# Background work between the score passes, and four kinds of small memory-layer operations on ScalarE

## Chip, cores and metric

The kernel runs on one core of a Trainium2 chip. The metric is device time in microseconds (us) for one execution, lower is better; for one core it is the time of that core. Engines are called as the profile calls them: PE is TensorE (PEld its weight loads), DVE is VectorE, ACT is ScalarE, POOL is GpSimd, SP is SyncE, whose queue issues nearly all transfers here.

## What is computed

Four transformer-like layers follow each other on one sequence of 2048 tokens of width 128, all in float32. Each half layer is `x = x + f(layernorm(x))`:

- L0: 16 heads of width 8 over the whole sequence, then a GELU network of 512.
- L1: 16 heads of width 64 over the whole sequence, then a gated network of 384. This attention is the longest stage.
- L2: attention of every token over itself and its two neighbours, then one of eight experts per token.
- L3: a memory layer and a mixture of experts. The memory layer cuts the sequence into 32 chunks of 64 tokens. In every chunk the gradient of a small two-layer network is taken at the state that the chunk before left, and three first-order recurrences along the tokens (with the gates `alpha`, `eta`, `theta`) make of it the state of the next chunk. So the 32 chunks are one serial chain:

```python
for c0 in range(0, S, CHUNK):
    g = _grad_fn(W_state, k[:, sl], v[:, sl]) * GRAD_SCALE
    ...
    (S_state, W_state), Wtraj = jax.lax.scan(step, (S_state, W_state), xs)
    ...
    outs.append(jnp.einsum('bto,btpo->btp', h, W2t))
```

The neighbours in L2 wrap round at the sequence's ends, so a block of tokens needs an edge token of the next block; those edge tokens are computed by themselves ahead of their blocks (the "late edge tokens", lines 1318 to 1374, which the change leaves as they are).

## The kernel before

**Stages.** L0 runs first, up to about 908 us. Then `l1_attn` (line 1066) runs the L1 attention as 40 units: five blocks of queries (512, 384 + 4 edge tokens, 512, 384 and 256 tokens) times eight pairs of heads. A unit has 16 steps, one for each 128 keys. In a step PE makes the scores of two heads, in four passes that add up in PSUM (query high part with key high part, query low part with key high part, query high part with key low part, and a row that subtracts the maximum); ACT takes the exponential into a `P` tile (line 1171); POOL adds the `P` tiles up into `acg`, or DVE into `acd` for four of the 16 steps (`do_sum`, line 1099); and two steps at a time PE multiplies `P` with the values (`do_pv`, line 1082). The maxima come one to two units early: extra products (`mi<-km,qh`) that DVE reduces into `mx` (`max_upto`, line 493).

**Background.** As soon as a block of queries is through all eight pairs of heads, its tokens can go on through the L1 network, L2 and L3. That is done by Python generators, called parts: `stage_a` to `stage_b2` for L1's network and L2, `stage_c` (line 1501) for what a block of 128 tokens needs ahead of the chunk chain, `chunk` (line 1630) for the chain, `stage_d` for its output, `stage_g`, `stage_e0`, `s_lane` and `stage_e1` for the experts. Each part is cut at every `yield` into pieces. What it yields tells the planner what comes next: a number is how many PSUM banks the next piece takes, "same" that it goes on on the same engine, "T" that it holds a product that needs no new bank, a fraction (only `T["late"]` = 0.3) how long to wait.

**What sets the order.** The program is scheduled by hand: each engine does its instructions strictly in the order in which the Python code emits them. A planner keeps a modelled clock for every engine (`note`, line 96) and `fill` (line 246) emits pieces whose inputs are ready by it. `Part.may` (line 202) is the gate; it also refuses a piece when ACT's or DVE's clock is too far ahead of PE's, and, during the attention, a piece that takes a bank unless five more banks stay free. `fill(lim, "t")` emits only pieces without a bank and without a product, and stops after `lim` us of PE's clock:

```python
if only and (self.banks or self.pe):
    return False
...
if len(free) < k + (0 if tail else leave[0]) or free[k - 1] > clk["T"] + T["slack"]:
```

All eight PSUM banks are one pool during the attention (`ps=dict(mx=8)`). In the loop over steps (lines 1136 to 1186) every second step, "last", calls a full `fill()` after its exponentials and another after its products with the values; each other step calls `fill(T["lim"], "t")` after its exponentials (line 1178). So the background comes in at three places in two steps. After the last unit `drain` (line 262) emits what is left; the stretch from there to the end is called the tail below.

**The lines that the prediction's steps touch.** In `stage_c`: the copies between `cb` (tile `sA`) and `hist` (lines 1526 and 1531), the copies of one column from `et` (tile `sB`) into `de` (tile `dE`) and from `om` (tile `sA`) into `do` (tile `dO`), each ahead of a memset of the column copied (lines 1600 to 1603), and the two products into `g1` (tile `gq`, lines 1619 to 1622). `stage_e0` (line 1876) takes a PSUM bank for a block's expert sum, which is given back only when all 13 weight tiles of the block have been through the lanes. Because a helper records every operation, the profile puts all of them on line 147, and they are told apart by their tiles.

Of the kernel before, what the change touches and what calls it, by code (L numbers as in the profile page):

```python
# [14 lines left out]
ALU = mybir.AluOpType  # L15
# [13 lines left out]
CH = 64  # L29
NCH = S // CH  # L30
ATANH = (1.0000000039388743, 0.3333315796754013, 0.20012426861749952, 0.13980709417165652, 0.14087328632693624)
T = dict(lead0=22, more0=4, mgap=0.4, pvq=2, lim0=0.5, fq=(3,), pl=-0.5, pr=1.0, tlow=2, tback=3, late=0.3, pvp="mx", mxp="mx", ex=(1280, 1792, 2047), low=1, lows='ge', keep=1, leave=5, pvn=2, sp=0, rdy=40., eu=2, qg=(22, 16, 10), em=2, el=6, sem=0.2, same=1.2, tsame=3.0, order="hdmBbAaEcCeg", ps=dict(mx=8), dma=2.3, slack=0.1, lim=0.6, backlog=2.5, lead=(10, 8, 6), pp=9, dve=(6, 7, 14, 15), qp=(1, 1), lanes=2, xl=5,
         QB=[(0, 512, 512), (512, 384, 388), (896, 512, 512), (1408, 384, 384), (1792, 256, 256)])


# [35 lines left out]
def body(ctx: ExitStack, tc: tile.TileContext, x, pa, pb, pc, pi, pd, pr, pr0, pe, pw, out):  # L71
# [16 lines left out]
    leave = [0]  # L88
# [92 lines left out]
    mxp = ["mx"]  # L181
# [12 lines left out]
    class Part:  # L194
# [24 lines left out]
        def step(self):  # L219
            piece[0] = clk["T"]  # L220
            r = next(self.gen, "end")
            self.same = r == "same"
            self.ready = 0.0 if self.same else piece[0] + (r if type(r) is float else 0.0)
            self.pe = r == "T"
            self.banks = r if type(r) is int else 0
            self.seen = len(emitted) if r is False else -1
            if r == "end":
                emitted.add(self.key)
            return r != "end"
# [16 lines left out]
    def fill(lim=None, only=""):  # L246

        t0 = clk["T"]
        while clk["T"] - t0 < (lim or T["lim"]):
            kept[0] = 0  # L250
            h = next((h for h in helpers if h.may(only)), None)
            if h:
                if not h.step():
                    helpers.remove(h)
                continue
            st = next((s for s in parts if s.may(only)), None)
            if st is None:
                return
            if not st.step():
                parts.remove(st)  # L260
# [20 lines left out]
    def mm(o, lhsT, rhs, start=True, stop=True, **kw):  # L281
        return te.matmul(o, lhsT, rhs, start=start, stop=stop, **kw)
# [740 lines left out]
    def stage_wo(qb, part):  # L1023

        t0, tn, n = QB[qb]
        yield 1
        ps = mi()
        for p in range(2 * part, 2 * part + 2):
            mm(ps[:, :n], C("wo", p * 128, 128), O.pop(p)[:, :n], start=(p % 2 == 0), stop=(p % 2 == 1))
            yield  # L1030
        if part == 0:
            w = l1w.tile([128, 512], F32, name="wac", tag="wac", bufs=1)
            se.activation(w[:, :n], ps[:, :n], AF.Identity, bias=bo1)
            rel(ps)
            wacc[qb] = w
            return
        w = wacc[qb]
        ve.tensor_tensor(w[:, :n], w[:, :n], ps[:, :n], ALU.add)
        rel(ps)
        if part < NP1 // 2 - 1:  # L1040
            return
        del wacc[qb]
        yield 1
        c0, nt = t0 // 128, tn // 128
        t = mi()
        for i in range(nt):
            te.transpose(tok(t, i), tok(w, i), ident)
        yield
        ve.tensor_tensor(xs[:, c0:c0 + nt, :], xs[:, c0:c0 + nt, :],
                         t[:, :tn].rearrange("p (c d) -> p c d", d=128), ALU.add)  # L1050
        rel(t)
        emitted.add(("x", qb))
        if n != tn:
            ne = len(EXTRA)
            xm = edge_x[0] = sm.tile([ne, 128], F32, name="xm", tag="xm", bufs=1)
            for i, t in enumerate(EXTRA):
                sy.dma_start(xm[i:i + 1, :], xs[t % 128:t % 128 + 1, t // 128, :])
            yield 1
            t = mi()
            te.transpose(t[:ne, :128], w[:, tn:tn + ne], ident)  # L1060
            yield
            ve.tensor_tensor(xm, xm, t[:ne, :128], ALU.add)
            rel(t)
            emitted.add("xm")

    def l1_attn():
# [15 lines left out]
        def do_pv(g, pts, v):  # L1082
            u, k = divmod(g, 16)
            n = QB[units[u][0]][2]
            if k == 0:
                pv[u] = take([T["pvp"]])
            for e in range(2):
                mm(pv[u][64 * e:64 * e + 64, :n], v[:, k % SPC, 64 * e:64 * e + 64], pts[e][:, :n],
                   start=(k == 0), stop=(k == 15), par=(e == 1))
            if k == 15:  # L1090
                accs = acc.pop(u)
                if u:
                    need(("o", u - 1))
                o = opool.tile([128, 512], F32, name="o", tag="o")
                se.copy(o[:, :n], pv[u][:, :n])
                rel(pv.pop(u))
                ends.append((u, o, accs))
# [38 lines left out]
        for g in range(16 * U):  # L1136
            u, k = divmod(g, 16)
            qb, p = units[u]
            n = QB[qb][2]
            if k == 0:  # L1140
                need(("m", u))
                need(("ql", u))
            if u + 2 < U:
                if k == 1 and units[u + 2][1] == 0:
                    need(("q", u + 1))
                    u_loadx(units[u + 2][0])
                if k == T["qp"][n <= 256] and u + 2 >= EU:
                    helper(("q", u + 2), u_qprep(u + 2))
            if k == 2 and 1 < u + 1 < U:
                need(("q", u + 1))  # L1150
                helper(("ql", u + 1), u_qlow(u + 1))
            if k % SPC == 0:
                ka, v = nxt.pop(0)
                g2 = g + 2 * SPC
                if g2 < 16 * U:
                    nxt.append(u_loadk(g2 // 16, (g2 % 16) // SPC))
            last = len(prev) == T["pvn"] or g == 0
            if not last:

                max_upto(max_at(g + 16 + LEAD[n] + 1))  # L1160
            pts = []
            ks = slice((k % SPC) * 128, (k % SPC) * 128 + 128)
            pss = [take(["mx"]) for _ in range(2)]
            ops = ((ka[:, 0, ks], qhh[u]), (ka[:, 0, ks], qlt[u % 2]), (ka[:, 1, ks], qhh[u]), (onr, mbt[u % 2]))
            for i, (a, b) in enumerate(ops):
                for e in range(2):
                    rows = slice(64 * e, 64 * e + 64)
                    mm(pss[e][:, :n], a[rows], b[rows, :n], start=(i == 0), stop=(i == 3), par=e and 0.02)
            for e in range(2):
                pt = pp.tile([128, 512], F32, name="P", tag="P")  # L1170
                se.activation(pt[:, :n], pss[e][:, :n], AF.Exp)
                rel(pss[e])
                pts.append(pt)
            if last:
                max_upto(max_at(g + 16 + LEAD[n] + 1))
                fill()
            else:
                fill(T["lim"], "t")
            if prev:
                do_sum(*prev[-1])  # L1180
            if len(prev) == T["pvn"]:
                while prev:
                    do_pv(*prev.pop(0))
                fill()
            do_merge()
            prev.append((g, pts, v))
        do_sum(*prev[-1])
# [313 lines left out]
    def stage_c(b):  # L1501
# [6 lines left out]
        ps = mi()  # L1508
# [14 lines left out]
            se.activation(th[:, k, :], pa_[:, 32 * k:32 * k + 32], AF.Tanh, scale=0.5, accum_out=s3[:, k:k + 1])  # L1523
        rel(ps)
        yield from wait(("hist", b - 1))
        ve.tensor_copy(cb[:, 0:3], hist)
        yield
        y = lt([128, BN3], "sB" + v)
        tap = lambda j, lo=0, hi=128: C("ctap", j, 1)[lo:hi]
        ve.tensor_scalar(y, cb[:, 0:BN3], tap(0), C("cb"), ALU.mult, ALU.add)  # L1530
        ve.tensor_copy(hist, cb[:, BN3:BN3 + 3])
        emitted.add(("hist", b))
        yield "same"
        for j in (1, 2):
# [62 lines left out]
                                ident[0:64, 0:64].unsqueeze(1).to_broadcast([64, BC3, CH]), ALU.mult, ALU.mult)  # L1597
        yield "same"
        ve.tensor_scalar(fl(om), ps[0:64, :BN3], -0.05 / 32, 0.95, ALU.mult, ALU.add)
        ve.tensor_copy(de[32:64, :, 0:1], et[32:64, :, 0:1])  # L1600
        ve.memset(et[:, :, 0:1], 0.0)
        ve.tensor_copy(do[0:32, :, 0:1], om[0:32, :, 0:1])
        ve.memset(om[:, :, 0:1], 0.0)
        yield "same"
        ve.tensor_tensor_scan(fl(h_), fl(et), fl(imp), 0.0, ALU.mult, ALU.add)
# [11 lines left out]
        yield "same"  # L1617
        ve.tensor_tensor_scan(ab, fl(om), fl(do), 0.0, ALU.mult, ALU.add)
        for r, t, k in ((slice(0, 64), ch(ab), 0), (slice(32, 64), do, 32)):
            ve.tensor_tensor(g1[r, :, k:k + 32], i1[r].unsqueeze(1).to_broadcast([r.stop - r.start, BC3, 32]),  # L1620
                             last(t)[r].to_broadcast([r.stop - r.start, BC3, 32]), ALU.mult)
        yield "same"
        qab = d["qab"] = lt([64, BN3], "qab", 3)
        ge.tensor_tensor(qab, qd_, ab, ALU.mult)
        kcs = d["kcs"] = lt([64, BC3, 2, 32], "kcs", 2)
# [4 lines left out]
    def chunk(b, c):  # L1630
# [46 lines left out]
        ve.tensor_tensor(ef, pf, v2f, ALU.subtract)  # L1677
        ve.tensor_tensor(e2, pt, kvt[:, c, 1, :], ALU.subtract)
        ve.scalar_tensor_tensor(u, tht, 2.0, u, ALU.mult, ALU.add)
        yield  # L1680
        mm(da, ef, w2)
        se.activation(j1, e2, AF.Square, accum_out=rr[:, 1:2])
        acs = lt([64, 2, 32], "acs", 1, l3c)
# [437 lines left out]
```

## Time and profile before

Three runs took 2908.26, 2917.2 and 2914.99 us; the median is 2914.99 us.

| | before |
|---|---|
| profiled execution, its own time | 2916.98 us |
| span in the profile | 2915.2 us |
| mean granted PE clock | 0.946 |
| busy: PE, DVE, ACT, POOL | 2681.3, 2247.1, 1552.2, 1365.5 us |
| attention steps of L1: first and last `mi<-mbt,onr` product | 907.9 and 2533.3 us |
| tail, from there to the end of the span | 382 us |
| share of PE and of DVE in the chain that ended last | 61% and 24% |

A unit issues 32 products `mi<-mbt,onr`, so counting them in the trace gives the start of each unit: unit 17 begins at 1551 us, unit 26 at 1976 us. The background is thin up to unit 16 and thick from there on.

A profile is of one execution. "PEclk" in it is the clock that PE was granted, 1.00 being full speed. A busy PE that runs at half speed shows as busy.

### The profile page before, as it was taken

The page shows a single profiled execution, that of the slowest core. Times are in us where ns is not written, and L with a number is a line of the kernel's source. Part 1 is how long each engine was busy: PE and PEld are TensorE (multiplying, and loading weights), DVE is VectorE, ACT ScalarE, POOL GpSimd, SP SyncE. Part 2 cuts the span into 40 slices and gives each one's busy share as a digit, 9 for nine tenths or more (in the row PEclk, how much of TensorE's full clock was granted, in tenths as well). Part 3 has the DMA queues.
Part 4 walks back from the last instruction along what each step waited for, and adds up shares of the span by engine and source line. Part 5 has one row for each costly group of instructions (what it writes and reads, how often), then busy time and mean ns, then how long its engine had stood idle before and what let it go on. Part 6 is the DMA issues. An engine that isn't in the chain of part 4 may idle for free.

```text
span 2915.2 us, 50126 instructions
## 1 busy us (share of the span) xinstructions
PE 2681.3 (92%) x16719; PEld 1361.4 (47%) x16719; DVE 2247.1 (77%) x4860; ACT 1552.2 (53%) x3932; POOL 1365.5 (47%) x1601
## 2 busy tenths in 40 slices
PE   7999999999988899999999999899889998879898
PEld 1222232222234444455554444455545565556676
DVE  7899888998643767777777778787788888787765
ACT  1788887887964454544444444344344344333444
POOL 3400110201114777766765766466556556433454
PEclk9999999999988999999999999999999999777879
DMA  6311231230225333344443333233233444222344
GB/s 146 74 28 17 52 109 18 73 91 16 79 83 179 100 112 114 120 120 122 139 133 95 97 97 96 81 106 105 92 96 114 122 121 116 79 57 75 80 112 117
DMA packets 247751, 275.82 MB, mean 95 GB/s; under 512 B 95747, under 2 KB 183330, under 8 KB 247366
## 3 DMA queue, kind: packets, MB, share of 16 engines
q1 hardware_dynamic: 246630, 272.43, 33.9%
q8 instruction: 133, 2.18, 0.3%
q14 instruction: 124, 1.02, 0.1%
q10 hardware_dynamic: 864, 0.20, 0.0%
HBM read 229.97 MB, written 42.28 MB: 93 GB/s over the span
## 4 chain that ended last, share of the span: by engine, by line
PE 61%; DVE 24%; ACT 6%; issue 4%; DMA 3%; POOL 1%; SPq 0%; ACTq 0%; POOLq 0%; DVEq 0%
PE mi L147 61%; DVE mx L147 8%; DVE acd L147 3%; ACT P L147 3%; DVE xn L147 1%; DVE xs L147 1%; DVE sB L147 1%; DMA rcd<-rc 1%; DVE gt L147 1%; DMA rb<-rcd 1%; ACT kf L147 1%; DVE hb L147 1%; ACT kh L147 1%; DVE bst L147 1%; DVE sG L147 1%
## 5 line engine op out<-in xcount | busy, mean ns | idle before, releaser
L147 DVE TENSOR_REDUCE mx<-mi 128x1 f32<-128x512 f32 (+1 forms) x2080 | 1318.8, 682 | 458.9 <-PE mi L147 447.5
L147 ACT ACTIVATE P<-mi 128x512 f32<-128x512 f32 (+3 forms) x2304 | 1118.3, 554 | 916.9 <-PE mi L147 891.9
L147 POOL TENSOR_TENSOR acg<-acg,P 128x512 f32<-128x512 f32 (+3 forms) x800 | 858.0, 1100 | 278.3 <-ACT P L147 277.9
L147 PE MATMUL mi<-P,ka 128*64 128x512 f32 (+3 forms) x2560 | 531.2, 537 | 1.9 <-ACT P L147 1.9
L147 PE MATMUL mi<-qh,ka 64*128 64x512 f32 (+3 forms) x2560 | 480.8, 363 | 25.1 <-DVE mx L147 13.7
L147 PE MATMUL mi<-kop,qop 48*128 48x512 bf16 x1024 | 347.5, 404 | 24.6 <-DVE mx L147 12.3
L147 PE MATMUL mi<-qop,kop 50*128 50x512 bf16 x1024 | 316.6, 389 | 27.1 <-ACT P L147 24.7
L147 PE MATMUL mi<-P,vop 128*32 128x512 f32 x2048 | 303.3, 618 | 13.9 <-ACT P L147 13.9
L147 PEld LDWEIGHTS mi<-qh,ka 64*128 64x128 f32 x2560 | 265.0, 189 | 94.4 <-issue 29.5
L147 PE MATMUL mi<-km,qh 64*128 64x512 f32 x1024 | 270.7, 459 | 36.3 <-DVE mx L147 28.8
L147 PEld LDWEIGHTS mi<-P,ka 128*64 128x64 f32 x2560 | 160.1, 140 | 244.2 <-issue 209.1
L147 PE MATMUL mi<-ql,ka 64*128 64x512 f32 (+3 forms) x1280 | 241.7, 354 | 0.0
L147 PE MATMUL mi<-mbt,onr 64*128 64x512 f32 (+3 forms) x1280 | 238.1, 351 | 0.4 <-DMA mbt<-mb 0.4
L147 POOL TENSOR_SCALAR vep<-mv 128x2 f32<-128x2 f32 (+1 forms) x24 | 5.5, 229 | 494.1 <-DVE mv L147 494.1
L147 PEld LDWEIGHTS mi<-km,qh 64*128 64x128 f32 x1024 | 118.6, 188 | 188.4 <-DVE mx L147 84.7
L147 PEld LDWEIGHTS <-kop 50*128 50x128 bf16 x1024 | 63.5, 95 | 303.6 <-issue 280.1
L147 POOL TENSOR_TENSOR acg<-P 128x512 f32<-128x512 f32 (+3 forms) x80 | 88.0, 1120 | 230.9 <-ACT P L147 135.0
L147 PEld LDWEIGHTS mi<-mbt,onr 64*128 64x128 f32 x1280 | 133.7, 189 | 11.2 <-DMA mbt<-mb 1.0
L147 PEld LDWEIGHTS mi<-ql,ka 64*128 64x128 f32 x1280 | 130.4, 189 | 13.5
L147 PEld LDWEIGHTS <-qop 48*128 48x128 bf16 x1024 | 73.0, 95 | 97.2 <-issue 82.8
L147 PEld LDWEIGHTS mi<-P,vop 128*32 128x32 f32 x2048 | 55.4, 109 | 119.4 <-issue 90.6
L147 POOL TENSOR_TENSOR kl<-kf,kh 128x512 f32<-128x512 f32 x32 | 40.9, 1277 | 111.5 <-ACT kh L147 83.0
(510 smaller groups left out, 3516.6 us busy)
## 6 DMA issues: line engine op xcount, KB each, us to landing
ka<-kvd SPq DMA_DIRECT2D x320, 384.0 KB
km<-khd SPq DMA_DIRECT2D x159, 256.0 KB
khd<-kh SPq DMA_DIRECT2D x32, 256.0 KB
kvd<-kh SPq DMA_DIRECT2D x32, 256.0 KB
kvd<-kl SPq DMA_DIRECT2D x32, 256.0 KB
kvd<-vt SPq DMA_DIRECT2D x16, 512.0 KB
w3s<-in_pw_dram SPq DMA_DIRECT2D x38, 192.0 KB
ka<-in_pw_dram SPq DMA_DIRECT2D x35, 192.0 KB
```

Of the source, the lines that this page charges most:

```text
L147: r = f(*a, **k)
```

## The change

Four things are changed, and nothing that is computed:

1. In the attention loop the parts' pieces without products may be emitted at many more places: after the first three of the four score passes, after the exponentials, after each step's product with the values, and after the full fill. Each such call has a limit of 9 us of PE's clock in place of 0.6. The full fills stay. The old call on the steps between is gone (its branch never runs).
2. Three kinds of piece that begin with a product are now marked so that these calls leave them out: the second product of `stage_wo`, the product `da` in `chunk`, and any piece after a fractional wait (the last products of a lane).
3. In `stage_c`, four copies and the products into `g1` go from DVE to ACT. [...]
4. After them the part yields plainly in place of "same".

```diff
-            self.pe = r == "T"
+            self.pe = r == "T" or type(r) is float
...
-            yield
+            yield "T" if p % 2 == 0 else 0
...
                     mm(pss[e][:, :n], a[rows], b[rows, :n], start=(i == 0), stop=(i == 3), par=e and 0.02)
+                if T["tf"] and i in T["ti"]:
+                    fill(9.0, "t")
...
-            else:
-                fill(T["lim"], "t")
+            elif 0:
+                fill()
+            if T["tf"]:
+                fill(9.0, "t")
             if prev:
                 do_sum(*prev[-1])
             if len(prev) == T["pvn"]:
                 while prev:
                     do_pv(*prev.pop(0))
+                    if T["tf"]:
+                        fill(9.0, "t")
                 fill()
+                if T["tf"]:
+                    fill(9.0, "t")
...
-        ve.tensor_copy(cb[:, 0:3], hist)
+        se.copy(cb[:, 0:3], hist)
...
-        ve.tensor_copy(hist, cb[:, BN3:BN3 + 3])
+        se.copy(hist, cb[:, BN3:BN3 + 3])
...
-        ve.tensor_copy(de[32:64, :, 0:1], et[32:64, :, 0:1])
+        se.copy(de[32:64, :, 0:1], et[32:64, :, 0:1])
         ve.memset(et[:, :, 0:1], 0.0)
-        ve.tensor_copy(do[0:32, :, 0:1], om[0:32, :, 0:1])
+        se.copy(do[0:32, :, 0:1], om[0:32, :, 0:1])
         ve.memset(om[:, :, 0:1], 0.0)
...
-            ve.tensor_tensor(g1[r, :, k:k + 32], i1[r].unsqueeze(1).to_broadcast([r.stop - r.start, BC3, 32]),
-                             last(t)[r].to_broadcast([r.stop - r.start, BC3, 32]), ALU.mult)
-        yield "same"
+            for c in range(BC3):
+                se.mul(g1[r, c, k:k + 32], i1[r], last(t)[r, c])
+        yield
...
         ve.scalar_tensor_tensor(u, tht, 2.0, u, ALU.mult, ALU.add)
-        yield
+        yield "T"
         mm(da, ef, w2)
```

The values added to the table of constants are `ti=(0, 1, 2)` and `tf=1`.

More of the change, by code (lines that the diff above doesn't have):

```diff
@@ L31 @@
 ATANH = (1.0000000039388743, 0.3333315796754013, 0.20012426861749952, 0.13980709417165652, 0.14087328632693624)
-T = dict(lead0=22, more0=4, mgap=0.4, pvq=2, lim0=0.5, fq=(3,), pl=-0.5, pr=1.0, tlow=2, tback=3, late=0.3, pvp="mx", mxp="mx", ex=(1280, 1792, 2047), low=1, lows='ge', keep=1, leave=5, pvn=2, sp=0, rdy=40., eu=2, qg=(22, 16, 10), em=2, el=6, sem=0.2, same=1.2, tsame=3.0, order="hdmBbAaEcCeg", ps=dict(mx=8), dma=2.3, slack=0.1, lim=0.6, backlog=2.5, lead=(10, 8, 6), pp=9, dve=(6, 7, 14, 15), qp=(1, 1), lanes=2, xl=5,
+T = dict(ti=(0, 1, 2), tf=1, lead0=22, more0=4, mgap=0.4, pvq=2, lim0=0.5, fq=(3,), pl=-0.5, pr=1.0, tlow=2, tback=3, late=0.3, pvp="mx", mxp="mx", ex=(1280, 1792, 2047), low=1, lows='ge', keep=1, leave=5, pvn=2, sp=0, rdy=40., eu=2, qg=(22, 16, 10), em=2, el=6, sem=0.2, same=1.2, tsame=3.0, order="hdmBbAaEcCeg", ps=dict(mx=8), dma=2.3, slack=0.1, lim=0.6, backlog=2.5, lead=(10, 8, 6), pp=9, dve=(6, 7, 14, 15), qp=(1, 1), lanes=2, xl=5,
          QB=[(0, 512, 512), (512, 384, 388), (896, 512, 512), (1408, 384, 384), (1792, 256, 256)])
```

## The prediction

> **What bounds the kernel now.** I read the totals first: PE is busy 92% of the span, so PE is the bound in name. Then the busy time by stretch: units 17 to 25, units 26 to 39, and the tail. Columns: start and end, length, then busy time of PE, PEld, DVE, ACT and POOL, the granted clock, the DMA share, GB/s.
>
> ```profile
> 1551.00:1976.00 425.00, 398.72 (x2353) 208.75 (x2349) 342.99 (x651) 184.44 (x459) 269.53 (x249) 0.98 0.32 96
> 1976.00:2533.00 557.00, 512.63 (x3788) 316.21 (x3787) 448.15 (x1109) 229.75 (x810) 329.75 (x455) 0.94 0.37 107
> 2533.00:2915.00 382.00, 328.30 (x1687) 247.06 (x1687) 277.41 (x1043) 156.90 (x641) 164.65 (x272) 0.80 0.36 87
> ```
>
> PE stands idle 425.0 - 398.7 = 26 us, 44 us and 54 us in the three, and loses by its clock 425 x 0.02 = 8 us, 557 x 0.06 = 33 us and 382 x 0.20 = 76 us. So 26 + 44 + 8 + 33 = 111 us of the attention with background, and 130 us of the tail, are not PE at its speed. The two losses belong together, as one stall shows. The timeline has DVE at three small operations that took 3.59 us (a `sB` operation of this form has a mean of 0.354 us), then PE that waits for `sA`, their successor:
>
> ```profile
> 1845.76 3.59 DVE L147 SCALAR_TENSOR_TENSOR sB<-sB,sA 128x32 f32<-128x32 f32 x3
> ...
> 1849.87 0.53 PE L147 MATMUL mi<-ident,s 128*64 128x128 f32 x2 [3.02 <-DVE sA L147]
> ```
>
> The granted clock of the next two 10 us was 0.83 and 0.86, after 1.00: a stall of 3 us was paid once as a stall and again, some 20 x 0.155 = 3 us, as clock.
>
> What PE waits for in the attention with background: the waits of PE alone in units 26 to 39 begin with
>
> ```profile
> PE mi L147 <- DVE mx L147: 15.6, 15, 3.0
> ```
>
> and for units 17 to 25 the same row has 17.9 us. Those 33.5 us of the 70 are waits for a PSUM bank that DVE has yet to reduce; the other 37 us are mostly waits for background results, nearly all from DVE. So DVE's lateness, through PE, is what a change can win here.
>
> Last, the rows of the operations that the change moves (ns minimum, median, maximum):
>
> ```profile
> L147 DVE COPY dE<-sB x16: 158/158/2592, 1857.4 to 2798.3; 32x2 f32<-32x2 f32 x16
> ...
> L147 DVE TENSOR_TENSOR gq<-i,ab x16: 216/217/754, 1861.6 to 2800.9; 64x64 f32<-64x64 f32 x16
> L147 DVE TENSOR_TENSOR gq<-i,dO x16: 215/530/3132, 1861.8 to 2801.1; 32x64 f32<-32x64 f32 x16
> ```
>
> The reader is to see that an operation of 0.2 us sometimes takes 2 to 3 us. It works no longer; it is held up while POOL is busy (the second product stands just behind POOL's `qab`, which reads the same tile).
>
> **Part 1: DVE to ACT.** Summed over the 16 calls of `stage_c`, the six removed DVE operations take 3.6 and 5.2 us (`hist`), 6.8 (`dE`), 3.9 (`dO`), 4.7 and 17.4 (`gq`): 41.6 us, of which 26.0 before 2533 us (nine calls) and 15.6 in the tail (seven). At their minima they would take 16 x (0.15 + 0.15 + 0.16 + 0.16 + 0.22 + 0.22) = 17 us; the other 25 us are hold-ups.
> In the attention the gain is between 0 (DVE was idle anyway: it waits 130 us for `mi` between 1551 and 2533) and all 26. I take half, **-13**, since DVE is busy 81% there and PE's waits are for DVE.
> ACT gets four copies and four products a call. Nearest rows: ACT's `ce` copies at 0.18 to 0.19 us, its products by a scale 0.20 (`ce`) to 0.32 us (`en`); so 4 x 0.19 + 4 x 0.26 = 1.8 us, 16 us in nine calls. ACT is busy 414 of 982 us there and waits 463 us for PE's scores, so its time costs nothing by itself; without that cover it would cost the 16.
> The new wait is DVE's: the memsets of `et` and `om` may not run until ACT has copied the column, and behind them on DVE stand the scans and the `mx` reductions that free PE's banks. It is no less than a copy and its hand-over, 0.3 us; with a pair of exponentials (2 x 0.55 us) ahead of it on ACT, 1.5 us. I take 0.5 a call, nearer the first, since the new places put the copy ahead of a step's exponentials: 9 x 0.5, **+4** (ends 3 and 14). `hist` needs no hand-over: ACT writes and reads it, and SP and POOL are not passed by any of these.
> In the tail the removed operations stand on the chain itself: 2.6 us of `dE` at 2531 and 0.4, 0.4, 1.7, 2.4 and 0.2 us of `gq`, together 7.7: **-7**. New waits there 7 x 0.5, **+3**.
>
> [...]
>
> **Part 2: the new places.** In the order of the two programs nothing differs in L0 and little in the first units; the background matmuls, counted by unit, are 157 in both up to unit 16; then 207 before and 293 after in units 17 to 25, 488 and 396 in units 26 to 39, 882 and 888 in the tail. DVE's background operations go from 308, 756 and 992 to 424, 570 and 958. So the background starts earlier and ends no earlier: work is moved from units 26 to 39 into units 17 to 25, and what is left for the tail is the same. Six matmuls of about 0.3 us less in the attention are **-2**, back in the tail as +2.
> What can be won is stalls. A DVE or ACT piece goes in as soon as it is ready, while a product still waits for a full fill; so between the piece and its product more foreground stands. No row shows this. At best the 37 us of waits for background results and half of the 41 us of lost clock vanish (-57); at worst ACT pieces ahead of exponentials delay `P`, for which PE waits 1.1 us now, and DVE pieces ahead of `mx` double the 33.5 us of bank waits (+34). I take a fifth of the first end, **-12**, since the waits to be shortened are the larger half.
>
> **Part 3: what the early start brings with it.** Since the first blocks reach `stage_g` early, `stage_e0` of block 0 is emitted in unit 26 in the changed order (before: in the tail), and it holds one of eight PSUM banks to the tail. Counted at the start of each step, 2.6 banks are held in units 26 to 29 against 2.2, and 2.5 against 1.8 in units 34 to 39. PE's bank waits after unit 26 are 15.6 us: from 0 (banks suffice) to double, with half of the 33 us of lost clock added (+32). I take **+6**.
> The chain of chunks enters the tail later: `stage_c` of block 7 was done in unit 39 and is now done after the last unit, and the tail has one `stage_c` and 0.8 `chunk` more (448 against 380 and 576 against 550 operations), two `stage_g` less. A chunk in the tail took (2847.6 - 2540.8) / 17 = 18 us by the ends of its `xst` copies. If the chain alone sets the tail, +18, and up to +27 if a whole attention-paced chunk is missing; if throughput does, 0. With PE 86% and DVE 73% busy there, I take a third: **+6**.
>
> Sum: -13 + 4 - 7 + 3 - 2 + 2 - 12 + 6 + 6 = -13. Against the profiled execution's 2917.0 that is **2904 us**; the median of the runs, 2915.0, is 2 us lower.
>
> **Rivals.**
> *Slower, about 2940.* The bank of `stage_e0` together with the later chain. Place: units 26 to 39 and the tail. Price: bank waits doubled with their clock, +32 in place of +6, and a whole chunk, +18 in place of +6; so -13 + 38 = +25. It decides once the two cost more than 25 together (they cost 12 in my sum). For it: 0.4 to 0.7 banks less; against it: 5.4 banks for scores and maxima are left.
> *Same, about 2916.* DVE behind ACT. If each copy stands behind one of ACT's 195 waits for scores (463 / 195 = 2.4 us), 16 x 2.4 = 38 us replace the +7, half of it on the path: +12. Against it: the places ahead of the exponentials. The same time comes out if the change does not do what it says and only moves work from late units to early ones (852 and 846 matmuls in the attention) without shortening a stall: then part 2's -12 falls away.
> *Much faster, about 2870.* Part 2 reaches four fifths of its 57 us in place of one: -46 for -12, so -47. For it: each stall of some 3 us that goes pays twice. Against it: no row shows how many of the waits were for pieces that a full fill had held back.
>
> **Chances.** Forecast with its surroundings (2892 to 2907) 0.3; much faster 0.2; same 0.2; slower 0.3. About 0.3%, 9 us, is what a measurement can tell from no change, so faster is 0.5, same 0.2, slower 0.3. The range reaches from 2859 (part 2 at its best end, -57) to 2954 (the slower rival with part 2 at nothing, +37); the forecast case alone is 2892 to 2907.
>
> **What would show it.** Part 1: no `gq` or `dE` in DVE's long operations, DVE's busy time some 40 us lower, and a short or long row "DVE sB or sA <- ACT dE or dO". Part 2: PE's waits for background results below 37 us, granted clock above 0.94 in units 26 to 39. Part 3: PE's waits for `mx` there above 15.6 us, first `xst` of the tail more than 8 us after the last step. I am wrong if DVE hands its hold-ups to its next operation, or if the tail is longer than 390 us.

## The result, and the profile after

The changed kernel took 2958.0 us (median; 2948.4 to 2963.7) against 2911.8 us for the kernel before on the same chips: the ratio is 1.0154, with a 95% interval of 1.0121 to 1.0187. It is 1.5% slower, where 0.4% faster was forecast, and lies just above the range (2859 to 2954).

The stretches of the changed kernel, cut by the same products as before (units 17 to 25, units 26 to 39, tail; columns as in the prediction):

```profile
1568.00:2032.00 464.00, 432.78 (x2514) 228.20 (x2510) 387.74 (x778) 205.63 (x562) 284.65 (x275) 0.94 0.30 88
2032.00:2570.00 538.00, 490.37 (x3613) 298.27 (x3613) 406.38 (x924) 232.97 (x760) 324.88 (x425) 0.94 0.41 115
2570.00:2962.00 392.00, 335.42 (x1697) 246.16 (x1695) 271.00 (x998) 172.47 (x721) 169.65 (x282) 0.78 0.34 78
```

Units 17 to 25 grew from 425 to 464 us (they have 86 background matmuls more), units 26 to 39 shrank from 557 to 538 (92 less), the tail grew from 382 to 392. That is +39 - 19 + 10 = +30. The rest of the 47 us that the profiled span grew lies in units 0 to 16, 19 us (662 in place of 643; what stands ahead of the attention was 2 us shorter), where the background has not even begun in earnest and where I had looked for nothing. Here the kernel before and then the changed one, units 0 to 7 and 8 to 16:

```profile
908.00:1229.00 321.00, 309.66 (x1846) 153.92 (x1848) 215.41 (x331) 153.01 (x301) 233.45 (x204) 0.98 0.38 116
1229.00:1551.00 322.00, 315.28 (x2168) 179.29 (x2166) 244.38 (x430) 153.68 (x377) 215.04 (x208) 0.99 0.43 125
```

```profile
906.00:1240.00 334.00, 314.04 (x1846) 155.16 (x1848) 220.48 (x331) 153.48 (x300) 233.33 (x204) 0.97 0.36 112
1240.00:1568.00 328.00, 317.68 (x2172) 179.36 (x2168) 245.38 (x431) 155.79 (x378) 213.24 (x207) 0.99 0.43 124
```

The same 1846 products in units 0 to 7, and 13 us more. The timeline of one of those units shows why. DVE in unit 3 of the kernel before, then of the changed one (start, duration, operation):

```profile
1054.10 2.94 DVE L147 TENSOR_TENSOR acd<-P 128x512 f32<-128x512 f32 x2
1056.97 1.27 DVE L147 TENSOR_REDUCE mx<-mi 128x1 f32<-128x512 f32 x2
1058.17 0.68 DVE L147 TENSOR_TENSOR o<-o,rb 128x512 f32<-128x512 f32 x1
```

```profile
1053.70 2.94 DVE L147 TENSOR_TENSOR acd<-P 128x512 f32<-128x512 f32 x2
1056.57 1.77 DVE L147 TENSOR_TENSOR o<-o,rb 128x512 f32<-128x512 f32 x1
1058.26 1.27 DVE L147 TENSOR_REDUCE mx<-mi 128x1 f32<-128x512 f32 x2
```

The product of a finished unit's `o` with its reciprocal sums (`rb`) is a piece of `u_end`, one of the helpers: generators like the parts, which serve the attention itself and which `fill` asks first. It now stands one step earlier: behind the two `acd` additions of step 8 and ahead of the two `mx` reductions for which PE waits. It also takes 1.77 us in place of 0.68. POOL adds into `acg` meanwhile (from 1056.53 us on), and I read the longer time as a hold-up by POOL; but POOL was adding over the whole of the 0.68 us in the kernel before too (from 1056.93 us on), and what lets the product through there is not shown. PE in that unit of the kernel before, then of the changed one:

```profile
1057.70 0.50 PE L147 MATMUL mi<-km,qh 64*128 64x512 f32 x1 [0.46 <-DVE mx L147]
1058.13 1.94 PE L147 MATMUL mi<-P,ka 128*64 128x512 f32 x8
```

```profile
1058.99 0.50 PE L147 MATMUL mi<-km,qh 64*128 64x512 f32 x1 [2.15 <-DVE mx L147]
1059.42 3.62 PE L147 MATMUL mi<-P,ka 128*64 128x512 f32 x8
```

It waits 2.15 us for `mx` where it waited 0.46 us before, and then its eight products take 3.62 us in place of 1.94, at half the clock. The unit is 42.1 us long in place of 38.7: the stall's 1.7 us, and 1.7 us of clock. Over the whole attention PE's waits for `mx` went from 49.8 to 78.0 us, and DVE's own waits for the transfer `rb` from 11.0 to 34.0. The latter, before and after:

```profile
DVE o L147 <- DMA rb<-rcd: 11.0, 10, 3.5
```

```profile
DVE o L147 <- DMA rb<-rcd: 34.0, 16, 6.4
```

So the new places brought a DVE piece forward to where DVE is already late, and what stands behind it in the order waits too: in unit 3 the `mx` reductions begin 4.56 us after the `acd` additions, in place of 2.87. The wait for the transfer is another matter. In units 2 to 6, where each of PE's stalls for `mx` grew by 1.7 us, DVE did not wait for `rb` at all; 14.6 of the 34.0 us lie in units 8 to 15 and 18.2 in units 27 to 39. What these waits cost by themselves is not separated here.

### The profile page after: what moved, and what is told of

The parts are those of the page before. It is cut to its first block, busy times and chain, and to the rows that moved or that the text cites. A ratio compares the mean times of both kernels' runs of the same rounds, so it can differ in the third digit from the quotient of the medians.

```text
span 2962.0 us, 50115 instructions
## 1 busy us (share of the span) xinstructions
PE 2705.1 (91%) x16719; PEld 1363.5 (46%) x16719; DVE 2249.5 (76%) x4756; ACT 1594.8 (54%) x4064; POOL 1378.8 (47%) x1609
## 4 chain that ended last, share of the span: by engine, by line
PE 47%; DVE 20%; DMA 5%; issue 4%; ACT 3%; POOL 1%; SPq 1%; POOLq 0%; DVEq 0%; ACTq 0%
PE mi L147 47%; DVE mx L147 6%; DVE acd L147 3%; DMA rcd<-rc 2%; DMA rb<-rcd 2%; DVE sB L147 1%; ACT P L147 1%; DVE o L147 1%; DVE xs L147 1%; DVE sG L147 1%; DVE gt L147 1%; DVE hb L147 1%; SPq L147 1%; DVE xn L147 1%; DVE sc L147 0%
## 5 line engine op out<-in xcount | busy, mean ns | idle before, releaser
L147 PE MATMUL mi<-P,ka 128*64 128x512 f32 (+3 forms) x2560 | 540.1, 544 | 2.6 <-ACT P L147 2.6
L147 PE MATMUL mi<-kop,qop 48*128 48x512 bf16 x1024 | 347.1, 404 | 24.8 <-DVE mx L147 12.3
L147 POOL TENSOR_TENSOR acg<-P 128x512 f32<-128x512 f32 (+3 forms) x80 | 97.6, 1240 | 208.0 <-ACT P L147 143.4
```

What stands on the lines that cost most here:

```text
L147: r = f(*a, **k)
```

## The experiments

Every ratio below is to the kernel before, in runs of the same chips. Lengths by stretch come from each run's trace; the kernel before has medians of 2908.8 to 2911.8 us in these sets of runs. The theories were: P, the new places cost; A, the move to ACT costs; H, the helpers at the new places cost; L, the load moved into units 17 to 25 costs; and my slower rival, the PSUM bank of `stage_e0`.

### The two halves of the change apart

**e1_places**, the new places without the move to ACT:

```diff
-        se.copy(cb[:, 0:3], hist)
+        ve.tensor_copy(cb[:, 0:3], hist)
...
-            for c in range(BC3):
-                se.mul(g1[r, c, k:k + 32], i1[r], last(t)[r, c])
-        yield
+            ve.tensor_tensor(g1[r, :, k:k + 32], i1[r].unsqueeze(1).to_broadcast([r.stop - r.start, BC3, 32]),
+                             last(t)[r].to_broadcast([r.stop - r.start, BC3, 32]), ALU.mult)
+        yield "same"
```

> The new places alone; the copies and the products into gq stay on DVE. Theory P (the loss comes from the new places: pieces emitted earlier stand ahead of mx reductions on DVE): 2945 to 2965 us, and units 0 to 16 still some 15 us longer than in the kernel before. Theory A (the loss comes from DVE and ACT waiting for each other after the move of the small operations): 2905 to 2920 us.

Measured: 2968.2 us, ratio 1.0179 (1.0144 to 1.0215), a little above what theory P expected; units 0 to 16 took 665 us against 643. **e2_act** is the other half, the kernel before with the diff's lines in `stage_c` only:

> The move of the four copies and of gq to ACT alone, with the old places. Theory P: 2895 to 2915 us, as little as my steps for the move gave (-13 by its own terms). Theory A: 2940 to 2960 us.

Measured: 2893.4 us, ratio 0.9939 (0.9917 to 0.9962). Theory A is out, P stands. The move wins 18 us by itself, and the new places lose about 56 to 65, without it and with it. e2_act is the fastest kernel of the study. Its totals:

```profile
PE 2674.5 (92%) x16719; PEld 1353.9 (47%) x16719; DVE 2223.7 (77%) x4766; ACT 1580.3 (55%) x4058; POOL 1366.5 (47%) x1599
```

DVE's busy time fell by 23.4 us (from 2247.1), not by the 41.6 us of the operations removed. Its stretches (units 17 to 25, units 26 to 39, tail) show where the time went:

```profile
1552.00:1971.00 419.00, 399.42 (x2363) 209.38 (x2361) 334.04 (x645) 189.01 (x483) 272.53 (x251) 0.98 0.34 97
1971.00:2530.00 559.00, 518.63 (x3834) 318.71 (x3836) 447.63 (x1102) 244.68 (x878) 332.44 (x458) 0.94 0.40 107
2530.00:2895.00 365.00, 315.14 (x1632) 235.62 (x1632) 263.03 (x961) 165.62 (x677) 161.20 (x264) 0.79 0.39 90
```

Against the kernel before the attention from unit 17 on is 4 us shorter and the tail 17. The order differs too, although no place was added: 16 chunks end in the tail in place of 18.

**e9_copies**: e2_act with the products into `gq` left on DVE, that is the first four `se.copy` lines alone.

> The kernel before with the four copies on ACT, but the products into gq left on DVE. The move of all gave 2893 us, -18. If the hold-ups of gq (22 us of the 42 us of DVE time) carry the gain: 2903 to 2912. If the copies ahead of the memsets do: 2890 to 2897.

Measured: 2904.9 us, ratio 0.9988 (0.9966 to 1.0010), no difference from the kernel before that can be told. So the `gq` products carry most of the gain in time. Whether they do so by their hold-ups or by the order that the planner makes without them is not separated: here 15 chunks end in the tail.

### Helpers at the new places

**e3_nohelp**: the added calls pass another mark, with which `fill` leaves the helpers out, and the old call is back:

```diff
-            h = next((h for h in helpers if h.may(only)), None)
+            h = next((h for h in helpers if h.may(only)), None) if only != "p" else None
...
-                    fill(9.0, "t")
+                    fill(9.0, "p")
...
-            elif 0:
-                fill()
+            else:
+                fill(T["lim"], "t")
```

> The changed kernel, but the helpers (the end of a unit, preparation of queries, the maxima's end) are emitted only at the old places; the parts of L1's network, L2 and L3 use the new ones. Theory H (the helpers at the new places are what costs, since their DVE operations wait for a transfer or stand ahead of mx): units 0 to 16 back to some 643 us (they took 660), DVE's waits for the transfer rb back from 34 to about 11 us, total 2930 to 2942. Theory L (the load: background packed into units 17 to 25 and the tail's later chain): 2950 to 2960 us, even where units 0 to 16 get shorter.

Measured: 2932.7 us, ratio 1.0054 (1.0020 to 1.0088); units 0 to 16 took 641 us, DVE waited 23.3 us for `rb` (not the 11 expected), and PE's waits for `mx` in the attention were 55.2 us, against 78.0 in the changed kernel. H is right by 25 us.

**e7_ohold** keeps one piece alone to the full fills:

```diff
             sy.dma_start(rb[64 * e:64 * e + 64, :n], rcd[u, e:e + 1, :n].to_broadcast([64, n]))
-        yield
+        yield "T"
```

> The changed kernel, but of the helpers one piece alone (the product of o with the reciprocal sums rb, on DVE) is kept to the full fills. If this piece is what lengthens units 0 to 16 (it stands behind the acd additions and ahead of mx, and waits for the transfer rb): units 0 to 16 at 641 to 648 us in place of 656 to 662, and 2935 to 2948 us in all. If it is the helpers' other pieces: no change, 2950 to 2962.

Measured: 2926.8 us, ratio 1.0045 (1.0024 to 1.0066), -31 us. But units 0 to 7 stayed at 335 us. The order shows that in them the edit did not do what I meant: in unit 3 the full fill that takes the piece is still that of step 8, behind the same two `acd` additions. It was early because the piece ahead of it, the reciprocal of the sums whose result goes out and comes back as `rb`, was early too (step 5 in place of 6). **e10_rcohold** holds both:

```diff
         sy.dma_start(sc[:np_, :, :w], smd[u, :, :n].rearrange("e (q w) -> q e w", w=w))
-        yield
+        yield "T"
```

> The changed kernel, with both late pieces of a unit's end (reciprocal of the sums, product of o with rb) kept to the full fills; in unit 3 they stand in steps 6 and 10 (before: 6 and 9; changed: 5 and 8; with o alone kept: 5 and 8). If o behind the acd additions of step 8 is what lengthens units 0 to 7: 320 to 323 us for them in place of 334, and 2912 to 2924 us in all. If not: 333 to 336 us and the 2927 of the kernel with o alone kept.

Measured: 2919.4 us, ratio 1.0043 (1.0025 to 1.0061), -39 us; units 0 to 7 took 321 us. DVE in unit 3 of this kernel:

```profile
1056.09 2.94 DVE L147 TENSOR_TENSOR acd<-P 128x512 f32<-128x512 f32 x2
1058.95 1.28 DVE L147 TENSOR_REDUCE mx<-mi 128x1 f32<-128x512 f32 x2
...
1061.56 1.62 DVE L147 TENSOR_TENSOR o<-o,rb 128x512 f32<-128x512 f32 x1
```

The `mx` reductions are ahead of `o` again. The product itself is as slow as in the changed kernel, and no one waits for it. In units 0 to 16 its position was the cost: they took 636 us in place of 662. DVE's waits for the transfer did not go with it, and 24.8 us of them lie in units 32 to 39:

```profile
DVE o L147 <- DMA rb<-rcd: 27.7, 13, 5.3
```

The rest of the gain has another place: units 26 to 39 took 508 us in place of 538 (PE's waits for `mx` 15.5 us in place of 27.6, granted clock 0.98 in place of 0.94), and the tail 410 in place of 392.

**e15_helponly** asks the reverse: the move to ACT, the old places for the parts, and the new places for the helpers alone.

```diff
-            st = next((s for s in parts if s.may(only)), None)
+            st = next((s for s in parts if s.may(only)), None) if only != "h" else None
...
-                    fill(9.0, "t")
+                    fill(9.0, "h")
...
-            elif 0:
-                fill()
+            else:
+                fill(T["lim"], "t")
```

> The move to ACT (2893 us alone) with the new places open to the helpers alone; the parts have the old places. If the helpers' early pieces cost by themselves: units 0 to 16 some 655 to 662 us in place of 645, and 2910 to 2930 us in all. If they cost only together with the early parts: 2893 to 2905.

Measured: 2941.6 us, ratio 1.0107 (1.0071 to 1.0142), +48 us over e2_act, and units 0 to 16 at 657 us. The helpers need no partner to cost this; the size is above what I expected.

### The held bank

**e4_noe0** lets `stage_e0` run only in the tail:

```diff
-            if b and not tail:
-                yield from wait(("l", b - 1))
+            yield from wait("tail")
...
     tail.append(1)
+    emitted.add("tail")
```

> The changed kernel, but stage_e0 may run only in the tail, so that no expert sum holds a PSUM bank in the attention. My slower rival (the bank and the later chain): units 26 to 39 shorter by 10 us or more and 2930 to 2945 us in all. If the bank does not matter: 2950 to 2962 us.

Measured: 2933.7 us, ratio 1.0087 (1.0060 to 1.0115), -24 us: the time that the rival wants, but not at its place. Units 26 to 39 got longer, 565 us, and the tail much shorter:

```profile
2033.00:2598.00 565.00, 517.45 (x3863) 318.90 (x3861) 458.06 (x1151) 254.84 (x918) 331.98 (x459) 0.94 0.40 108
2598.00:2926.00 328.00, 278.73 (x1452) 213.59 (x1452) 227.75 (x785) 149.78 (x562) 150.18 (x237) 0.84 0.39 97
```

With the bank free, 531 background matmuls pass the planner's gate in units 26 to 39 in place of 396, and 12 chunks are left for the tail in place of 18.

**e12_bank7** takes a bank away from e2_act, with nothing else changed:

```diff
+            if g == 16 * 26:
+                bank["mx"].remove(min(bank["mx"]))
...
     tail.append(1)
+    bank["mx"].append(clk["T"])
```

> The kernel with the move to ACT alone (2893 us), with one of the eight PSUM banks left unused from unit 26 to the tail: the held bank by itself, without new places. Background matmuls there go from 506 to 349, chunks left for the tail from 16 to 22. If a held bank costs by keeping background out of the attention: units 26 to 39 some 50 us shorter, the tail some 90 us longer (six chunks more at 17 us, the wait for the lanes gone), 2920 to 2945 us. If the tail takes the work in without loss: 2893 to 2905.

Measured: 2937.6 us, ratio 1.0100 (1.0065 to 1.0136), +44 us over e2_act. Units 26 to 39 and the tail:

```profile
1971.00:2470.00 499.00, 465.09 (x3542) 282.22 (x3541) 371.09 (x817) 218.85 (x712) 308.87 (x402) 0.96 0.46 119
2470.00:2941.00 471.00, 389.95 (x1925) 281.81 (x1923) 327.85 (x1248) 195.27 (x848) 186.46 (x320) 0.74 0.32 71
```

The 157 matmuls that the gate kept out save 558.4 - 499.2 = 59 us in the attention, 0.38 us each, and cost 471.3 - 365.8 = 106 us in the tail, 0.67 us each. There they are links of the chunk chain: 22 chunks end in the tail in place of 16, and six more at 16.6 us each are 100 us. PE's waits for `mx` there did not grow (11.0 us in e2_act, 10.2 here). So the bank costs through what the planner lets in and not through PE lacking it.

**e11_leave4** opens the gate by one bank while the sum is held:

```diff
         ac = mi()
+        if not tail:
+            leave[0] -= 1
```

> The changed kernel, but while stage_e0 holds its bank the planner asks for four free banks and not five ahead of a background piece. Background matmuls in units 26 to 39 go from 396 to 579, chunks left for the tail from 18 to 10. If the held bank cost by the planner's gate alone: 2925 to 2945 us, as with stage_e0 in the tail. If PE really lacks the bank: its waits for mx after unit 26 grow by 15 us or more and it takes 2950 us or more.

Measured: 2952.5 us (2930.5 to 2963.8), ratio 1.0146 (1.0080 to 1.0212). Neither expectation fits. The waits for `mx` fell (20.3 us after unit 26 against 27.6 in the changed kernel), so PE did not lack the bank; with the bank free, in e4_noe0, they were 19.6 us. But units 26 to 39 took 601 us and the tail 319: +62 and -72 against the changed kernel. With 10 chunks left, a chunk of the tail took 21.7 us in place of 16.9, and 98 us passed from the last chunk to the end, in place of 66. I read this as the experts' lanes setting the end, so that further background in the attention buys nothing; no run shows it apart. The spread of this kernel is wide, its time cannot be told from the changed kernel's, and I would not put a figure on it.

### Both repaired, and what is left to the places between the passes

**e6_both** is e3_nohelp with e4_noe0; **e8_both_nopass** is that with `ti=()`, no places between the passes; **e5_nopass** is the changed kernel with `ti=()`.

> The changed kernel with the helpers at the old places and with stage_e0 only in the tail. Each alone gave about -25 us against the changed kernel. If the two causes add up (helpers ahead of mx in every unit; a bank that keeps background products out of units 26 to 39): 2905 to 2912 us, units 0 to 16 some 641 us, a tail near 325 us. If they share a cause: 2925 to 2935. If the new places for the other parts are a gain by themselves, it ends below the 2893 of the move to ACT alone.

> As the kernel with both repairs, but without the places between the score passes; those after the exponentials, after each product with the values and after the full fill stay. If the places between the passes are of use to the parts: 5 to 20 us more than the kernel with both. If they load units 17 to 25 without a gain: the same or 5 to 15 us less.

> The changed kernel without the places between the score passes; the others stay, with helpers, and stage_e0 still holds its bank. Between the passes cost 21 us in the kernel with both repairs (2924.6 against 2903.4). If that is a price of the places themselves: 2930 to 2942 us here. If it was only that more background there buys nothing once the lanes set the end of the tail: 2950 to 2962 us here, where 18 chunks are left for the tail with and without them.

Measured: 2924.6 us, ratio 1.0041 (1.0018 to 1.0065); 2903.4 us, ratio 0.9970 (0.9949 to 0.9990); and 2954.2 us, ratio 1.0153 (1.0118 to 1.0187). The repairs gave -33 us together and not -49, and without the places between the passes another -21; yet the changed kernel itself gains only 4 without them.

The last two take the finer repair: **e13_all** is e10_rcohold with e4_noe0, **e14_all_nopass** that with `ti=()`.

> The changed kernel with both late pieces of a unit's end kept to the full fills and stage_e0 in the tail. If the two causes add up fully: 2919 - 24 = 2895 us, as good as the move to ACT alone. If they share work, as the kernel with helpers at the old places and stage_e0 in the tail did (2924.6): 2905 to 2925 us.

> As the last, without the places between the score passes. Background matmuls left for the tail are 772 against 771 and chunks 12.0 against 12.75, so no work is moved to or from the tail. If the places between the passes cost by themselves: 10 to 25 us less than the last. If they cost only by moving work that the tail takes in for nothing: the same within 6 us.

Measured: 2904.2 us, ratio 0.9978 (0.9959 to 0.9996), and 2917.5 us, ratio 1.0030 (1.0008 to 1.0052). Holding two pieces and one stage back brings 54 of the 65 us between the changed kernel and e2_act; the separate effects, 39 + 24, add up to 9 us more, which is within the spread of these runs. And here, where neither expectation fits, the places between the passes are worth 13 us, against -21 with e6_both and e8_both_nopass. Their own worth has no settled sign. In e6_both 543 background matmuls stand in units 26 to 39 and 746 in the tail, in e8_both_nopass 531 and 795, with the same tail of 334 us, so there they only moved work in front of a tail that took it in for nothing; why they help in e13_all stays open, as does where its last 11 us over e2_act lie.

## Why the prediction was wrong

**Part 1 had the sign and nearly the size, and not the place.** The move gave -18 us; my terms were -13 + 4 - 7 + 3 = -13. But of these the attention was to give 9 us and the tail 4, and e2_act won 4 us in the attention from unit 17 on and 17 in the tail, with two chunks less there, a change of order that no term had. So it is partly luck that the sum came near. The new wait was smaller than I thought: DVE behind ACT's copies of `dE` was 2.5 us in three waits up to the tail in e2_act, where I had 4.

Whether the hold-ups go with the operations that are moved, or pass to other DVE operations, has an answer nearer the second. Of 41.6 us removed, 23.4 stayed gone, not much above the 17 us that the minima alone would give; so by DVE's total some 18 of the 25 us of hold-ups came back on other operations, which I had named as a sign of being wrong. For `dE` the hold-ups came while POOL was busy: in the kernel before, the ten copies during which POOL was idle took 0.16 us each, the six others 0.24 to 2.59 us. A part of what came back shows on another DVE operation: `kcs`, which follows in the part, went from at most 0.41 us to at most 1.22 us and from 4.6 to 8.3 us in all. Before, then e2_act:

```profile
L147 DVE TENSOR_TENSOR kcs<-kvt,ce x16: 273/280/406, 1868.0 to 2803.6; 64x128 f32<-64x128 f32 x16
```

```profile
L147 DVE TENSOR_TENSOR kcs<-kvt,ce x16: 252/276/1218, 1852.8 to 2754.0; 64x128 f32<-64x128 f32 x16
```

In the changed kernel, which has the move too, the six calls of `kcs` above 0.3 us (0.33 to 1.34 us) all overlap an operation of POOL, two of them `qab`. Where the other 14 us came back was not followed. I had also read `qab` as what holds up the second product into `gq`. Beside `qab` alone it took 0.38 us; where it took 3.13 us in the kernel before, four additions of POOL into `acg` followed on `qab`, and the product ended just behind the last of them:

```profile
2376.64 3.13 DVE L147 TENSOR_TENSOR gq<-i,dO 32x64 f32<-32x64 f32 x1
2376.91 2.78 POOL L147 TENSOR_TENSOR acg<-acg,P 128x256 f32<-128x256 f32 x4
```

**Part 2 failed, at its step "I take a fifth of the first end, -12".** The gain that I saw exists, and is small: PE's idle time for other reasons than `mx` fell from 37 us (70.7 less 33.5) to 30 us (78.9 less 49.1) between unit 17 and the tail. The loss, which I had as the other end, "DVE pieces ahead of `mx` double the 33.5 us of bank waits", was larger: PE's waits for `mx` went from 33.5 to 49.1 us there, and from 16.4 to 28.9 us in units 0 to 16, which the step left out because the background is thin there. Units 17 to 39, before and after, then units 0 to 16:

```profile
PE mi L147 <- DVE mx L147: 33.5, 33, 4.3
```

```profile
PE mi L147 <- DVE mx L147: 49.1, 36, 6.5
```

```profile
PE mi L147 <- DVE mx L147: 16.4, 18, 7.1
```

```profile
PE mi L147 <- DVE mx L147: 28.9, 27, 7.1
```

What I had missed is that the helpers are background too. They are in every unit, most of their pieces hold no product, and one of them, brought forward by a step, stands between the slow `acd` additions and the `mx` reductions. I had counted pieces by unit and found units 0 to 16 equal, 157 and 157; the count was right, and the order within a unit was what changed. That was in the built order to be read. e10_rcohold prices the two pieces of `u_end` at 39 us in the changed kernel, e15_helponly the helpers at 48 us with the move alone. So the new places, with the bank of part 3, cost 65 us where parts 2 and 3 together had 0.

My price for a stall's clock was also misread. The 3 us were summed over 20 us, and the second ten of them (0.86) hold the drop to 0.50 from 1867.1 us on, during a later stall, of 4.25 us for `mx`, that ended at 1868.9 us. The first ten alone give 10 x 0.17 = 1.7 us, which is what unit 3 of the changed kernel shows.

**Part 3 had the mechanism and not its size or its way.** The bank of `stage_e0` costs 24 us in the changed kernel (e4_noe0), where I took +6 and +6 for the bank and the later chain. I priced it by PE's waits for `mx`, and those after unit 26 did rise, from 15.6 to 27.6 us. That rise is not the bank's price: e12_bank7 shows the bank's cost without any rise, and in e10_rcohold the waits are back at 15.5 us although `stage_e0` still runs in the attention there (its first product stands at 2123 us). The bank costs through the gate and the chain. The chain did enter the tail later: the first `xst` of the tail came 38.2 us after the last step in place of 7.4, 31 us more. But the chunks were then faster, 16.9 us in place of 18.0, which over 17 of them is 19 us, and the tail grew by 10 us, between my +6 and the +18 of "if the chain alone sets the tail". Why the chunks were faster is not shown; two stages of other work were already done by then. At 392 us the tail is also past the 390 that I had named as a sign of being wrong.

**The rivals.** The slower one, at 2940, named one of the two true causes and the right sign, for the wrong reason, and lacked the helpers. The others found no support: DVE behind ACT cost next to nothing, and part 2 brought a loss and not four fifths of its 57 us. The change did shorten the stalls that it could shorten, by the 7 us above, and paid for it elsewhere.

## What to carry to other kernels

- Where each engine keeps a strict order, an earlier place for an operation is worth something only if nothing that the bound engine needs stands behind it; look at what is directly ahead of it and behind it on its own engine, above all where that engine is already late.
- A count of operations by stage does not show a reordering within the stage: compare one period, line by line, before and after.
- Where a planner makes the order from modelled times, moving an operation to another engine also changes the order: read the gain by stretch before you put it down to the operation.
- When background work is gated by a scarce buffer, price a held buffer by the work that no longer passes the gate and by what that work costs where it lands, not only by the bound engine's waits for the buffer.

## What the runs showed of the hardware

After three of five PE waits of 2.15 us for `mx` the granted clock was 0.50. Units 2 to 6 of the changed kernel each have one of the five. In units 2 and 4 it cost only its own 1.7 us, in units 3 and 5 it cost 3.4 and in unit 6 3.1. In these five cases it goes by where the wait falls. In the traces of the kernel before and of the changed one the granted clock is 1.00 or 0.50 and changes only at points of a grid of 3.41 us. In units 3, 5 and 6 all of the wait lies inside one piece of the grid, and PE ran at 0.50 for the next piece; in units 2 and 4 a point of the grid cuts it in two (1.04 and 1.12 us, 1.55 and 0.60 us), and the clock stayed at 1.00. Three pieces around the wait of unit 2, then two around that of unit 3 (the last three columns are clock, DMA share and GB/s):

```profile
1011.76:1015.17 3.41, 2.37 (x19) 1.59 (x17) 3.41 (x3) 2.06 (x4) 2.98 (x3) 1.00 0.60 195
1015.17:1018.58 3.41, 2.19 (x7) 0.82 (x9) 3.04 (x6) 0.00 (x0) 3.41 (x3) 1.00 0.00 0
1018.58:1021.99 3.41, 3.41 (x20) 1.39 (x16) 0.59 (x1) 0.69 (x1) 0.62 (x1) 1.00 0.29 96
```

```profile
1056.13:1059.54 3.41, 1.26 (x10) 0.54 (x8) 3.40 (x4) 1.72 (x4) 3.01 (x3) 1.00 0.46 169
1059.54:1062.95 3.41, 3.41 (x8) 0.59 (x8) 1.38 (x3) 0.00 (x0) 2.37 (x2) 0.50 0.00 0
```

So in these five cases a piece with up to 1.55 us of the wait was followed by a clock of 1.00, and a piece with all 2.15 us by 0.50. No limit that holds elsewhere is shown: in the kernel before, a piece with 1.1 us of waiting for `mx` was followed by 0.50 too. There, the piece and the next:

```profile
1880.78:1884.20 3.42, 2.30 (x16) 1.40 (x17) 2.92 (x8) 2.30 (x6) 2.00 (x4) 1.00 0.42 158
1884.20:1887.61 3.41, 3.41 (x10) 0.87 (x7) 1.54 (x4) 0.55 (x5) 1.74 (x3) 0.50 0.00 0
```
